# A four-layer fp32 network on one core: layer 3's end with the next batch's scan outputs and the last batch's closing put beside the convolutions

## The chip, the core and the metric

One NeuronCore of one Trainium2 chip runs the whole network in one launch. The metric is the device time of that launch in microseconds. Three runs of the kernel before gave 16581.78, 16579.15 and 16575.54 us (median 16579.15).

## What is computed

The network takes `x` of shape (4, 96, 56, 56) through four layers, each on a normalised input: an attention layer, a layer of selective scans in eight directions, a layer of local top-k similarity with a feed-forward part, and the last one, "layer 3", whose end is changed here. For each of the four batches, layer 3 has four scans `y1..y4` over the image (two along rows, two along columns), each 192 wide per position. Its end, shortened from the reference:

```python
ys = (y1 + y2 + y3 + y4)                      # with Ds added to each
yn = (yn - mu) / jnp.sqrt(var + 1e-05) * ln_g + ln_b      # over the 192
u = jnp.moveaxis(yn, -1, 1) * z               # z: 1x1 projection of the layer's input
t = jax.nn.relu(bn(conv2d(u, c1_w, c1_b), ...))           # 192 -> 384
t = jax.nn.relu(bn(conv2d(t, c2_w, c2_b, groups=2*E, pad=1), ...))   # depthwise 3x3
t = conv2d(t, c3_w, c3_b)                     # 384 -> 96
s = t.mean((2, 3)); s = jax.nn.relu(s @ se1_w.T + se1_b)
s = jax.nn.sigmoid(s @ se2_w.T + se2_b)
return t + t * s[:, :, None, None]            # then added to the network's running x
```

All data are 32-bit floats.

## The kernel before

The four layers run one after the other. `layer3` first calls `into_layer3` (projection and a depthwise convolution) and `cumulative` (the scans, which leave their outputs `ys[0..3]` in DRAM, stored with position as the row and 192 values in a row). Then comes the stage of this document. It works on an image of 56 x 56 = 3136 positions in 7 chunks of 448 (`NCH`, `CH`), each chunk being 4 tiles of 112 positions (`KT`). Batches follow each other strictly, and each has two parts.

`gathered(b)` works with positions on partitions. Per chunk, SP's queue issues six loads for four tiles `y0..y3` (L1495 for the two row scans, L1501, twice each, for the two column scans); VectorE adds the four (L1505) and the constant `dsum` (L1506); `norm_rows` takes statistics (L777, L778), ScalarE a square root (L780), VectorE the reciprocal, the subtraction and multiplication (L784) and the norm's weight and bias (L788, L789). TensorE makes the gate `z` from the layer's input `xn`, which was loaded for the whole image (L1487, L1511); VectorE multiplies (L1512); TensorE transposes (L1516); ScalarE copies the result into `g`, channels on partitions (L1520). The pool of the `y` tiles has 3 buffers of each.

`bottleneck(b)` has NM = 3 tiles `m` of 128 channels. `convolve` runs over these tiles, one ahead: for chunk `c` it issues the depthwise taps of the tile before and the first 1x1 convolution ("fill") of the present tile. Of the nine taps, `on_pe` = 4 are TensorE matmuls with diagonal weights (L417, diagonals made at L403), and the other five are VectorE operations that read the image from SBUF and accumulate in the same PSUM tile (L422). The fill is two matmuls (L1531) and a ScalarE Relu (L1535) into a padded image `xp`; `ended` is a ScalarE Relu from the PSUM tile into `t2` (L1541). After the last tile the third convolution runs (L1557: three matmuls per chunk, L1558), then the mean and the two small matrices with a sigmoid (L1562 to L1572), and the output: VectorE forms `t3 * gate + x` (L1576) with `x` loaded for the whole image before the convolutions (L1524), and GpSimd's queue issues the store (L1577).

What sets the order: inside `in_order` each engine's instructions keep the order of the program text. In the kernel before, this holds for `convolve` only; `gathered` and the end of `bottleneck` are placed by the scheduler. All pools of a batch are opened and closed with it. `convolve` is also used by layers 1 and 3's beginnings, with 4 taps on TensorE there before and after.

Of the kernel before, what the change touches and what calls it, by code (L numbers as in the profile page):

```python
# [17 lines left out]
L = H * W  # L18
# [18 lines left out]
def flat(t):  # L37
    return t.rearrange("p a b -> p (a b)")
# [31 lines left out]
class Net:  # L70
# [319 lines left out]
    def convolve(self, tiles, two, sp, ps):  # L390

        nc = self.nc
        on_pe = 4
        for j in range(len(tiles) + 1):
            now = tiles[j] if j < len(tiles) else None
            old = tiles[j - 1] if j > 0 else None
            if now is not None:
                now["xp"] = two[j % 2]  # L400
                dg = now["dg"] = sp.tile([128, on_pe, 128], F32, name="dg")
                for k in range(on_pe):
                    nc.vector.tensor_scalar(  # L403
                        dg[:, k, :], self.ident, now["weights"][:, k : k + 1], None, ALU.mult
                    )
            for c in range(NCH):
                if old is not None:
                    xp, w = old["xp"], old["weights"]

                    def tap(k):  # L410
                        y = 8 * c + k // 3
                        return xp[:, y : y + 8, k % 3 : k % 3 + W]

                    p = ps.tile([128, 512], F32, name="d")
                    q = p[:, :CH].rearrange("p (h w) -> p h w", w=W)
                    for k in range(on_pe):
                        nc.tensor.matmul(q, old["dg"][:, k, :], tap(k), start=k == 0, stop=k == on_pe - 1)  # L417
                if now is not None:
                    now["fill"](c, now["xp"][:, 1 + 8 * c : 9 + 8 * c, 1 : W + 1])
                if old is not None:  # L420
                    for k in range(on_pe, 9):
                        nc.vector.scalar_tensor_tensor(q, tap(k), w[:, k : k + 1], q, ALU.mult, ALU.add)  # L422
                    old["ended"](c, q)

    def into_scan(self, xin, dram, orders):
# [7 lines left out]
        with ExitStack() as cx:  # L433
# [19 lines left out]
            def tile_of(pr, j):  # L453
# [46 lines left out]
                return dict(weights=cw[:, j, :], fill=fill, ended=ended)  # L500
# [520 lines left out]
    def into_layer3(self, xin, dram):  # L1021
# [4 lines left out]
        with ExitStack() as cx:  # L1026
# [19 lines left out]
            def tile_of(pr, j):  # L1046
# [41 lines left out]
                return dict(weights=cw[:, j, :], fill=fill, ended=ended)  # L1088
# [357 lines left out]
    def layer3(self, xin, xout, dram):  # L1446
# [4 lines left out]
        with ExitStack() as cx:  # L1451
            wp = cx.enter_context(tc.tile_pool(name="ow", bufs=1))
            ga = cx.enter_context(tc.tile_pool(name="og", bufs=1))
            ps = cx.enter_context(tc.tile_pool(name="op", bufs=3, space=PSUM))
            psz = cx.enter_context(tc.tile_pool(name="oz", bufs=1, space=PSUM))
            psd = cx.enter_context(tc.tile_pool(name="od", bufs=3, space=PSUM))
            wz = wp.tile([C, DI], F32, name="wz")
            nc.sync.dma_start(wz, self.d["l3_win"][:, DI : 2 * DI])

            lng, lnb, ds = (self.load_rows(wp, n) for n in ("l3_lnw", "l3_lnb", "l3_d"))  # L1460
            dsum = wp.tile([KT, DI], F32, name="dsum")
# [22 lines left out]
            def gathered(b, g, sp, ss):  # L1484

                xn = sp.tile([C, L], F32, name="xn")
                nc.sync.dma_start(xn, xs[b])  # L1487
                for t0 in range(0, NKT, 4):
                    four = [KT, 4, DI]
                    yk = []  # L1490
                    for k in range(4):
                        y = ss.tile(four, F32, name=f"y{k}")
                        if k < 2:
                            src = ys[k][b, t0 * KT : (t0 + 4) * KT, :].rearrange("(t p) d -> p t d", p=KT)
                            nc.sync.dma_start(y, src)  # L1495
                        else:
                            for r in range(2):
                                src = ys[k][b].rearrange("(w h) d -> w h d", h=H)[
                                    :, 2 * t0 + r : 2 * t0 + r + 7 : 2, :
                                ]  # L1500
                                nc.sync.dma_start(y[r * W : (r + 1) * W], src)  # L1501
                        yk.append(y)
                    acc = yk[0]
                    for k in (1, 2, 3):
                        nc.vector.tensor_tensor(acc, acc, yk[k], ALU.add)  # L1505
                    nc.vector.tensor_tensor(acc, acc, spread(dsum, 4), ALU.add)  # L1506
                    self.norm_rows(acc, lng, lnb, ss)
                    z = psz.tile([KT, 4, 256], F32, name="z")
                    for i in range(4):
                        at = (t0 + i) * KT  # L1510
                        nc.tensor.matmul(z[:, i, :DI], xn[:, at : at + KT], wz, start=True, stop=True)  # L1511
                    nc.vector.tensor_tensor(acc, acc, z[:, :, :DI], ALU.mult)  # L1512
                    for dh in range(2):
                        p = ps.tile([128, 512], F32, name="pn")
                        for i in range(4):
                            nc.tensor.transpose(  # L1516
                                p[:96, i * KT : (i + 1) * KT], acc[:, i, 96 * dh : 96 * dh + 96],
                                self.ident[:KT, :KT],
                            )
                        nc.scalar.copy(g[:, dh, t0 * KT : (t0 + 4) * KT], p[:96, : 4 * KT])  # L1520

            def bottleneck(b, g, sp, s1, ss):
                x = s1.tile([C, L], F32, name="x")
                nc.sync.dma_start(x, xin[b])  # L1524
                t2 = s1.tile([128, NM, L], F32, name="t2")

                def tile_of(m):
                    def fill(c, dst):
                        p = ps.tile([128, 512], F32, name="pn")
                        for dh in range(2):  # L1530
                            nc.tensor.matmul(  # L1531
                                p[:, :CH], c1[:, dh, m * 128 : (m + 1) * 128],
                                g[:, dh, c * CH : (c + 1) * CH], start=dh == 0, stop=dh == 1,
                            )
                        nc.scalar.activation(  # L1535
                            dst, p[:, :CH].rearrange("p (h w) -> p h w", w=W),
                            AF.Relu, bias=s1h[:, m : m + 1], scale=s1c[:, m : m + 1],
                        )

                    def ended(c, p):  # L1540
                        nc.scalar.activation(  # L1541
                            t2[:, m, c * CH : (c + 1) * CH], flat(p),
                            AF.Relu, bias=s2h[:, m : m + 1], scale=s2c[:, m : m + 1],
                        )

                    return dict(weights=c2[:, m, :], fill=fill, ended=ended)

                two = self.padded(s1)
                with in_order(tc):
                    self.convolve([tile_of(m) for m in range(NM)], two, sp, psd)  # L1550
                t3 = s1.tile([C, L], F32, name="t3")
                sums = ss.tile([C, NCH], F32, name="sums")
                for c in range(NCH):
                    cs = slice(c * CH, (c + 1) * CH)
                    p = ps.tile([128, 512], F32, name="pn")
                    for m in range(NM):
                        nc.tensor.matmul(p[:C, :CH], c3[:, m, :], t2[:, m, cs], start=m == 0, stop=m == NM - 1)  # L1557
                    nc.scalar.activation(  # L1558
                        t3[:, cs], p[:C, :CH], AF.Identity, bias=c3b, accum_out=sums[:, c : c + 1]
                    )  # L1560
                mean = ss.tile([C, 1], F32, name="mean")
                nc.vector.tensor_reduce(mean, sums, AX.X, ALU.add)  # L1562
                nc.vector.tensor_scalar(mean, mean, 1.0 / L, None, ALU.mult)
                p = ps.tile([128, 512], F32, name="pn")
                nc.tensor.matmul(p[: DI // 4, 0:1], se1, mean, start=True, stop=True)
                h1 = ss.tile([DI // 4, 1], F32, name="h1")
                nc.scalar.activation(h1, p[: DI // 4, 0:1], AF.Relu, bias=se1b)
                p = ps.tile([128, 512], F32, name="pn")
# [4 lines left out]
                for c in range(NCH):  # L1573
                    cs = slice(c * CH, (c + 1) * CH)
                    o = ss.tile([C, CH], F32, name="o")
                    nc.vector.scalar_tensor_tensor(o, t3[:, cs], gate, x[:, cs], ALU.mult, ALU.add)  # L1576
                    nc.gpsimd.dma_start(xout[b][:, cs], o)  # L1577

            for b in range(B):
                g = ga.tile([96, 2, L], F32, name="g")  # L1580
                with ExitStack() as c2x:
                    sp = c2x.enter_context(tc.tile_pool(name="ob", bufs=1))
                    ss = c2x.enter_context(tc.tile_pool(name="os", bufs=3))
                    gathered(b, g, sp, ss)
                with ExitStack() as c2x:
                    sp = c2x.enter_context(tc.tile_pool(name="tb", bufs=2))
                    s1 = c2x.enter_context(tc.tile_pool(name="t1", bufs=1))
                    ss = c2x.enter_context(tc.tile_pool(name="ts", bufs=3))
                    bottleneck(b, g, sp, s1, ss)
# [141 lines left out]
```

## Time and profile before

| | us |
|---|---|
| median of three runs | 16579.15 |
| the profiled execution | 16544.92 |
| its span | 16543.1 |
| last store of the scans issued | 15721.5 |
| first load of the stage issued (`wz`) | 15722.9 |
| end of the span | 16543.1 |

The stage lasts some 821 us of the span. The page gives busy time over the whole span: TensorE 13366.7 us (81%), VectorE 13918.8 (84%), ScalarE 12240.4 (74%), GpSimd 7665.0 (46%). In the rows, PE is TensorE, DVE VectorE, ACT ScalarE, POOL GpSimd and SP the queue that issues most loads; "PEclk" is the granted clock of TensorE as a share of its full speed. A group row gives the line, engine, operation, tiles written and read, shapes, count, busy time, mean duration of one in ns, and the idle time before it with what ended it. A 32-bit matmul leaves two records in the trace, so "x8" in a row of TensorE is four matmuls.

### The profile page before, as it was taken

How to read it: one execution, taken by the hardware profiler on the slowest of the kernel's cores; microseconds unless marked ns; L12 is line 12 of the kernel's file. 1: busy time of each engine (PE TensorE's matmuls, PEld its weight loads, DVE VectorE, ACT ScalarE, POOL GpSimd, SP SyncE). 2: the span in 40 equal slices, each digit the busy share in tenths (PEclk: the TensorE clock that was granted, in tenths of full speed). 3: DMA queues.
4: the chain of work that ended last, by engine and by line, in shares of the span. 5: the costliest groups of instructions: out<-in, count | busy, mean ns of one | idle time of the engine just before them, and what ended most of it. 6: DMA issues, size and time to landing. Idle time of an engine off the chain costs nothing.

```text
span 16543.1 us, 501276 instructions
## 1 busy us (share of the span) xinstructions
PE 13366.7 (81%) x221976; PEld 8983.6 (54%) x221976; DVE 13918.8 (84%) x15345; ACT 12240.4 (74%) x15452; POOL 7665.0 (46%) x3968
## 2 busy tenths in 40 slices
PE   8999977777777777777776678778888888888866
PEld 4333325666666666666665445446666656666533
DVE  7666549999999999999998777768888888888866
ACT  0465449999999999999996244468888888888822
POOL 0000028888888888888885000023333333333300
PEclk6899889999999999999998588889999999999977
DMA  0000034334444434344445800122212222221122
GB/s 15 1 1 1 16 137 97 91 92 95 105 105 103 103 91 96 92 96 102 103 105 139 194 10 10 43 71 51 50 47 50 50 50 51 51 50 47 43 66 66
DMA packets 821402, 1152.50 MB, mean 70 GB/s; under 512 B 309360, under 2 KB 728720, under 8 KB 807456
## 3 DMA queue, kind: packets, MB, share of 16 engines
q1 hardware_dynamic: 759872, 1055.38, 26.3%
q10 hardware_dynamic: 53984, 45.77, 1.2%
q8 instruction: 1745, 28.59, 0.8%
q0 software_dynamic: 5376, 19.27, 0.4%
q14 instruction: 425, 3.48, 0.1%
HBM read 842.93 MB, written 277.18 MB: 68 GB/s over the span
## 4 chain that ended last, share of the span: by engine, by line
PE 32%; DVE 28%; ACT 19%; issue 15%; DMA 5%; SPq 1%; POOL 1%; DVEq 0%; ACTq 0%; POOLq 0%
DVE q L638 17%; PE q L1357 7%; ACT ht L663 5%; PE s L233 4%; ACT e L626 3%; PE d L417 3%; ACT phi L1305 3%; DVE w L1345 3%; PE z L1297 2%; PE acc L251 2%; PE m L196 2%; ACT w L1313 2%; PE t L561 2%; PE y L675 2%; DVE phi L1366 2%
## 5 line engine op out<-in xcount | busy, mean ns | idle before, releaser
L618 POOL TENSOR_TENSOR q<-du,bm 128x1792 f32<-128x1792 f32 x1344 | 5345.3, 4024 | 3.1 <-DMA bm<-bc 3.1
L638 DVE TENSOR_TENSOR_SCAN q<-e,state,q 128x448 f32<-128x448 f32 x4608 | 4874.1, 1122 | 142.7 <-ACT e L626 140.1
L626 ACT ACTIVATE e<-dl,na 128x448 f32<-128x448 f32 x5376 | 3355.4, 640 | 179.4 <-DVE q L638 123.7
L675 PE MATMUL y<-ht,cd 128*32 128x64 f32 x75264 | 1836.6, 225 | 1480.0 <-ACT ht L663 1479.5
L654 PE MATMUL t<-ident,q 128*128 128x128 f32 x18816 | 2611.9, 292 | 93.9 <-issue 77.8
L1357 PE MATMUL q<-w,m 32*32 32x192 f32 x52224 | 2573.2, 348 | 124.1 <-DVE phi L1366 71.2
L654 PEld LDWEIGHTS t<-ident,q 128*128 128x128 f32 x18816 | 2377.1, 203 | 324.4 <-issue 201.1
L663 ACT COPY ht<-t 128x896 f32<-128x896 f32 x2688 | 2428.3, 903 | 87.1 <-PE t L654 57.1
L675 PEld LDWEIGHTS y<-ht,cd 128*32 128x32 f32 x75264 | 1399.7, 110 | 1958.2 <-ACT ht L663 1942.9
L1357 PEld LDWEIGHTS q<-w,m 32*32 32x32 f32 x52224 | 1873.3, 113 | 737.7 <-issue 184.3
L1366 DVE TENSOR_TENSOR phi<-q,phi 128x768 f32<-128x768 f32 x1632 | 1512.4, 952 | 519.4 <-PE q L1357 491.7
L1378 POOL TENSOR_TENSOR t<-t 128x384 f32<-128x384 f32 x408 | 407.3, 998 | 2974.2 <-DVE t L1377 2974.2
L1297 PE MATMUL z<-ad,sm 32*32 32x256 f32 x39168 | 1277.4, 391 | 396.2 <-ACT phi L1305 382.0
L241 ACT ACTIVATE e<-s 128x896 f32<-128x896 f32 (+1 forms) x1050 | 921.7, 915 | 902.6 <-PE m L196 508.2
L1305 ACT COPY phi<-z 128x1536 f32<-128x1536 f32 x816 | 1164.5, 1427 | 526.5 <-PE z L1297 526.3
L208 DVE TENSOR_REDUCE pm<-m 128x1 f32<-128x448 f32 (+1 forms) x1672 | 982.9, 616 | 667.1 <-PE m L196 599.6
L1345 DVE TENSOR_TENSOR w<-w,misc 128x3072 f32<-128x3072 f32 x408 | 1364.8, 3345 | 82.7 <-PE misc L1329 47.0
L1313 ACT ACTIVATE w<-phi,lntiny,w_k_rmask 128x3072 f32<-128x3072 f32 x408 | 1203.1, 2949 | 2.6
L196 PE MATMUL m<-ka,qa 32*128 32x448 f32 (+1 forms) x3344 | 1169.3, 638 | 7.5 <-DVE pm L208 7.5
L1321 ACT ACTIVATE phi<-phi,w_k_nmask 128x3072 f32<-128x3072 f32 x408 | 1165.5, 2857 | 2.4
L1297 PEld LDWEIGHTS z<-ad,sm 32*32 32x32 f32 x39168 | 708.7, 104 | 659.6 <-ACT phi L1305 463.0
L292 POOL DMA_DIRECT2D x<-xc x28 | 14.5, 517 | 2178.4 <-DVE xc L291 2177.5
(255 smaller groups left out, 18928.9 us busy)
## 6 DMA issues: line engine op xcount, KB each, us to landing
bm<-bc SPq DMA_DIRECT2D x896, 448.0 KB
cm<-cd SPq DMA_DIRECT2D x544, 186.0 KB
l1y<-out SPq DMA_DIRECT2D x672, 96.0 KB
l1y<-out SPq DMA_DIRECT2D x672, 72.0 KB
y<-l1y ACTq DMA_DIRECT2D x224, 168.0 KB
l3y<-y SPq DMA_DIRECT2D x1616, 23.2 KB
w<-l3cr SPq DMA_DIRECT2D x408, 48.0 KB
l3cr<-phi SPq DMA_DIRECT2D x408, 48.0 KB
```

What stands on the lines that cost most here:

```text
L618: nc.gpsimd.tensor_tensor(q, spread(s["du"][:, j, :], ng), s["bm"][g], ALU.mult)
L626: nc.scalar.activation(e[:, :CH], s["dl"][:, j, :], AF.Exp, scale=na[:, s["k"], j, n : n + 1])
L638: nc.vector.tensor_tensor_scan(a, e, a, first, ALU.mult, ALU.add)
L654: nc.tensor.transpose(flat(t)[:, 128 * c : 128 * c + 128], view(q, h * NC2 + c, [[NC, 128]]), self.ident,)
L663: nc.scalar.copy(t, flat(s["t", j, g, h])[:, : NC2 * 128])
L675: nc.tensor.matmul(s["y", j][r : r + 32, c // 4, 64 * half : 64 * half + 64], s["cd"][:, half, g, c, :], s["t", j, g, h][:, 128 * i + 64 * ...
L1297: nc.tensor.matmul(z[32 * b : 32 * b + 32, p, dh].rearrange("p n d -> p (n d)"), s["s"][ps_, dh, b, lo : lo + 32], st["ad"][ps_, dh, 8 * h ...
L1305: nc.scalar.copy(st["phi"][:, :, :, 8 * h : 8 * h + 8, :].rearrange("p a b n d -> p a b (n d)"), z.rearrange("p a b n d -> p a b (n d)"),)
L1313: nc.scalar.activation(w.rearrange("p a n d -> p (a n d)"), st["phi"].rearrange("p a b n d -> p (a b n d)"), AF.Sigmoid, bias=lntiny, scal ...
L1345: nc.vector.tensor_tensor(st["w"], st["w"], ut, ALU.mult)
L1357: nc.tensor.matmul(qp[bs, n, :DI], st["m"][bs, 4 * q + n, :], st["w"][bs, :, 4 * q + n, :], start=True, stop=True,)
L1366: nc.vector.tensor_tensor(ph, view(st[q], 0, [[256, 4], [32, 6], [1, 32]]), ph, ALU.mult)
```

## The change

All of the stage is now one `in_order` region with one set of pools. `gathered(0)` runs alone, as before. Then one call of `convolve` covers the twelve tiles of all four batches (13 rounds of 7 steps), and at each step it calls `before()`, which advances the closing of the batch before, and `beside()`, which advances the shaping of the next batch's scan outputs by one of three parts. The four scans are added by GpSimd. The weight of the norm goes into `wg` and its bias is brought in by one more matmul (`wz` times bias) in the PSUM tile where the transposes land; the transposes are ordinary matmuls with the identity. The subtraction and scaling go to ScalarE. The `y` tiles have 2 buffers, PSUM pools are smaller, and taps on TensorE are 3, 2, 3 for the tiles m = 0, 1, 2 in place of 4. `x` and `xn` are loaded chunk by chunk.

```diff
-    def convolve(self, tiles, two, sp, ps):
+    def convolve(self, tiles, two, sp, ps, before=lambda: None, beside=lambda: None):
...
             for c in range(NCH):
+                before()
                 if old is not None:
-                    xp, w = old["xp"], old["weights"]
+                    xp, w, on_pe = old["xp"], old["weights"], old["on_pe"]
...
                     old["ended"](c, q)
+                beside()
...
-            ps = cx.enter_context(tc.tile_pool(name="op", bufs=3, space=PSUM))
+            ss = cx.enter_context(tc.tile_pool(name="os", bufs=2))
+            ps = cx.enter_context(tc.tile_pool(name="op", bufs=2, space=PSUM))
             psz = cx.enter_context(tc.tile_pool(name="oz", bufs=1, space=PSUM))
-            psd = cx.enter_context(tc.tile_pool(name="od", bufs=3, space=PSUM))
+            pst = cx.enter_context(tc.tile_pool(name="ot", bufs=2, space=PSUM))
+            psd = cx.enter_context(tc.tile_pool(name="od", bufs=2, space=PSUM))
...
+            wg = wp.tile([C, DI], F32, name="wg")
+            nc.vector.tensor_tensor(wg, wz, lng[:C], ALU.mult)
+            nc.vector.tensor_tensor(wz, wz, lnb[:C], ALU.mult)
...
+            def fetch(b, c):
...
+                xn = ss.tile([C, CH], F32, name="xn")
+                nc.sync.dma_start(xn, xs[b][:, c * CH : (c + 1) * CH])
...
+            def added(q):
+                y = q["ys"]
+                nc.gpsimd.tensor_tensor(y[0], y[0], y[1], ALU.add)
+                nc.gpsimd.tensor_tensor(y[2], y[2], y[3], ALU.add)
+                nc.gpsimd.tensor_tensor(y[0], y[0], y[2], ALU.add)
+                nc.gpsimd.tensor_tensor(y[0], y[0], spread(dsum, 4), ALU.add)
+
+            def statistics(q):
...
+                    nc.vector.bn_stats(st[:, i, :], acc[:, i, :])
+                    nc.vector.bn_aggr(mv[:, i, :], st[:, i, :])
...
+                nc.scalar.activation(rs, mv[:, :, 1], AF.Sqrt, bias=self.eps[:KT])
+
+            def normalised(q):
...
+                    nc.tensor.matmul(
+                        z[:, i, :DI], q["xn"][:, i * KT : (i + 1) * KT], wg, start=True, stop=True
+                    )
+                nc.vector.reciprocal(rs, rs)
...
+                nc.vector.scalar_tensor_tensor(nm, mv[:, :, 0], -1.0, rs, ALU.mult, ALU.mult)
+                for i in range(4):
+                    nc.scalar.activation(
+                        acc[:, i, :], acc[:, i, :], AF.Identity,
+                        bias=nm[:, i : i + 1], scale=rs[:, i : i + 1],
+                    )
+
+            def gated(q):
+                acc = q["ys"][0]
+                nc.vector.tensor_tensor(acc, acc, q["z"][:, :, :DI], ALU.mult)
+
+            def turned(q):
...
+                for dh in range(2):
+                    p = pst.tile([128, 512], F32, name="tr")
+                    nc.tensor.matmul(
+                        p[:96, :CH], wz[:, 96 * dh : 96 * dh + 96], q["xn"], start=True, stop=False
+                    )
                     for i in range(4):
...
+                        nc.tensor.matmul(
+                            p[:96, i * KT : (i + 1) * KT], acc[:, i, 96 * dh : 96 * dh + 96],
+                            self.ident[:KT, :KT], start=False, stop=i == 3,
+                        )
+                    nc.scalar.copy(gs[b][:, dh, c * CH : (c + 1) * CH], p[:96, :CH])
+
+            def gathered(b):
+
+                qs = [fetch(b, 0), fetch(b, 1)]
+                added(qs[0])
+                for c in range(NCH + 1):
+                    if c < NCH:
+                        statistics(qs[c])
+                    if c > 0:
+                        turned(qs[c - 1])
+                    yield
+                    if c == NCH:
+                        return
+                    normalised(qs[c])
+                    if c + 1 < NCH:
+                        added(qs[c + 1])
+                    yield
+                    gated(qs[c])
+                    if c + 2 < NCH:
+                        qs.append(fetch(b, c + 2))
+                    yield
...
+                return dict(weights=c2[:, m, :], on_pe=(3, 2, 3)[m], fill=fill, ended=ended)
+
+            def closing(b):
+
                 t3 = s1.tile([C, L], F32, name="t3")
                 sums = ss.tile([C, NCH], F32, name="sums")
+                yield
                 for c in range(NCH):
...
+                        nc.tensor.matmul(
+                            p[:C, :CH], c3[:, m, :], t2[b, m][:, cs], start=m == 0, stop=m == NM - 1
+                        )
                     nc.scalar.activation(
                         t3[:, cs], p[:C, :CH], AF.Identity, bias=c3b, accum_out=sums[:, c : c + 1]
                     )
+                    yield
...
-                    o = ss.tile([C, CH], F32, name="o")
-                    nc.vector.scalar_tensor_tensor(o, t3[:, cs], gate, x[:, cs], ALU.mult, ALU.add)
+                    o = ss.tile([C, CH], F32, name="o", bufs=3)
+                    nc.sync.dma_start(o, xin[b][:, cs])
+                    yield
+                    nc.vector.scalar_tensor_tensor(o, t3[:, cs], gate, o, ALU.mult, ALU.add)
                     nc.gpsimd.dma_start(xout[b][:, cs], o)
...
+                for b in range(B):
+                    coming = closing(b - 1) if b > 0 else iter(())
+                    for _ in range(NM * NCH):
+                        next(coming, None)
+                        yield
+                yield from closing(B - 1)
+
+            ends = ending()
+            outputs = (x for b in range(1, B) for x in gathered(b))
+
+            with in_order(tc):
+                for _ in gathered(0):
+                    pass
+                self.convolve(
+                    [tile_of(b, m) for b in range(B) for m in range(NM)], two, sp, psd,
+                    lambda: next(ends, None), lambda: next(outputs, None),
+                )
+                for _ in ends:
+                    pass
```

## The prediction

> **What bounds the kernel now.** The change lies behind the scans, so I cut the stage first, by the table of windows (per row: length, then busy us and instructions of PE, PEld, DVE, ACT, POOL, then granted clock, DMA share, GB/s).
>
> ```profile
> 15722.00:15807.00 85.00, 29.36 (x111) 25.66 (x112) 65.86 (x161) 9.77 (x23) 0.00 (x0) 0.54 0.57 141
> 15807.00:15924.00 117.00, 113.92 (x301) 56.06 (x299) 73.12 (x114) 38.01 (x61) 0.77 (x8) 0.98 0.05 11
> 16327.00:16410.00 83.00, 29.57 (x114) 25.70 (x115) 66.25 (x152) 10.06 (x22) 2.94 (x12) 0.56 0.58 144
> 16410.00:16524.00 114.00, 112.06 (x297) 54.90 (x295) 72.90 (x111) 36.36 (x58) 0.23 (x3) 0.99 0.04 11
> ```
>
> Shaping (some 84 us a batch) is VectorE's, with TensorE a third busy at half clock; convolving and closing (some 117) is TensorE's. The chain of waits says the same of the second part:
>
> ```profile
> 15879.02 3.01 PE d L417 x8
> 15882.03 1.50 PE pn L1531 x4
> 15883.54 18.04 PE d L417 x48
> 15905.34 15.05 PE pn L1557 x40
> 15935.46 10.02 DMA y<-l3y
> ```
>
> A middle step is 3.01 + 1.50 = 4.51 us of TensorE: 0.75 per tap or per 448-wide matmul. The next batch's first loads start only after the closing, and 10 us of it show. The groups of the stage (the fourth of the whole page) give the prices of what moves:
>
> ```profile
> L1505 DVE TENSOR_TENSOR y<-y,y 112x768 f32<-112x768 f32 x84 | 79.6, 948 | 46.8 <-DMA y<-l3y 46.8
> L784 DVE TENSOR_SCALAR y<-y,mv,rs 112x192 f32<-112x192 f32 x112 | 34.8, 374 | 0.3
> L788 DVE TENSOR_TENSOR y<-y,w_l_lnw 112x768 f32<-112x768 f32 x28 | 26.6, 951 | 0.1
> L1228 POOL TENSOR_TENSOR du<-dl,u 96x752 f32<-96x752 f32 x136 | 244.2, 1796 | 30.2 <-ACT dl L1191 29.8
> ```
>
> Three rows of the timeline (start, length, work, count) give the pace of taps on VectorE, of short matmuls at full clock and of z at half clock:
>
> ```profile
> 15886.65 24.54 DVE L422 SCALAR_TENSOR_TENSOR d<-xp,w_l_c,d 128x448 f32<-128x448 f32 x35 [0.93 <-PE d L417]
> 10002.08 1.20 PE L999 MATMUL misc<-wt,ft 112*96 112x112 f32 x10 [0.52 <-ACT wt L996]
> 15801.55 2.77 PE L1511 MATMUL z<-wz,xn 96*112 96x192 f32 x8
> ```
>
> A tap on VectorE is 24.54 / 35 = 0.70. The stage is 821 us (15722 to 16543); everything else keeps its time.
>
> **Part by part.** *Off VectorE:* per chunk four adds (0.95 each), four L784, L788 and L789: 28 x (3.8 + 1.25 + 1.9) = some 195 us. What stays per chunk: statistics 1.35 (timeline: 0.33 per pair), two tiny operations 0.45, the gate's product 0.95, so 2.75. *On ScalarE:* 112 scalings of 112x192, not shown before; between L780 (112x4, 0.30) and L1193 (96x376, 0.48), I take 0.38: 43 us on an engine that has under 40 of 117 busy; off the path except before the product. *On GpSimd:* 112 adds of 112x768; nearest is L1228, 1.83 after scaling by 768/752, so 7.3 per chunk. *On TensorE:* z at full clock: in the last row above 8 records take 2.4 us at clock 0.54, so 1.3. Turning: two matmuls of 448 (1.5) and sixteen records of L999's very shape, 0.105 warm: 1.7, together 3.2. The other bound is z's 0.16 a record: 4.1, which would add some 0.9 per chunk beside m = 0 and in the chain, 12 x 0.9 = 11 in all; L999 is the nearer shape. At the cold clock I take 0.2 a record and, with the first long matmul done ahead, 4.6 after the product. The two `wg` products (0.36 each by L1462) lie under the first load.
>
> *A step with nothing to wait for.* m = 0 (3 taps on TensorE): per three steps VectorE has 18 x 0.70 + 0.3 + 2.75 = 15.7, TensorE 3 x (2.26 + 1.50) + 1.3 + 3.2 = 15.8: 5.25 a step. m = 1 (2 taps): VectorE 14.7 + 0.3 + 2.75 = 17.7, TensorE 13.5: 5.9. Moving taps to VectorE costs; the shaping under it pays.
>
> *The new chain.* The third convolution of a chunk is issued at the head of the step that follows its last tap tile. Its third matmul waits for that step's `ended`; in TensorE's order the next taps and fill stand behind it. So seven steps of each batch run in series: matmul 0.75, three taps 2.26 + 0.28 to the first VectorE tap, six taps 4.3, `ended` 0.72, handing over 0.15 (my guess; 0 to 0.4 would be 31 x 0.25 = 8 at most) = 8.45. Under it fits the fill, z and the other matmuls (4.3 of 5.2 free); turning overruns by 1.0, twice a batch. Before, these seven convolutions took 15 us a batch, so this is the dear part.
>
> *The loads.* SP now issues seven loads a chunk, the first waiting until the same buffer's earlier chunk is turned; 28 loads of `xn` (before 4) and 28 of `o` (before 4 of `x`) share that queue. From the second batch: 15931.36 to 15942.33 for 1.89 MB, then 1.5 and 1.8 us for the next two 0.344 MB: 2.0 fixed and 0.21 MB/us. So y3 lands 8.6 after release, three adds of GpSimd follow (5.5): 14 us from turned to statistics, on which all of VectorE's taps then wait. Beside m = 0, VectorE reaches them 20 us after the product, which is 17.4 after turning: covered with 3.3 to spare; m = 1, 6.1. Alone, in `gathered(0)`, it is not: turning 4.6, load and adds 14, statistics to product 4.9 = 23.5 per two chunks, against some 17 before. First chunk ready at 15743.5, last turned at 15823.5 (before: 15807); then seven fill steps wait on batch 1's first chunks, and the first tap of VectorE is at about 15850 (before 15823.5).
>
> *Outputs.* `o` is loaded on SP behind such a waiting fetch, twice in batches 1 and 2. It lands some 10 us after turning, VectorE wants it 3 us after: 7 us each, all its taps queued behind; bounds 0 (served at once) and 9. The sigmoid's table (1.28) and `ended` before it hold VectorE 2.3 per batch. At the end each third output waits for a store (2.4, the page's time from issue to landing), then a load: 12.5 from gate to last product, against 7.
>
> *One rule against it:* the Trainium skill, "SBUF — State Buffer", section "Who interferes with whom", says a VectorE instruction with two SBUF inputs and a GpSimd one that reads SBUF exclude each other for a whole instruction. The taps read one image from SBUF and one from PSUM, and layer 1's rows show them with GpSimd copying:
>
> ```profile
> 2292.44 3.59 DVE L422 SCALAR_TENSOR_TENSOR d<-xp,w_l_cw,d 128x448 f32<-128x448 f32 x5 [0.28 <-PE d L417]
> 2294.14 11.46 POOL L494 COPY t<-dup 128x3136 f32<-128x3136 f32 x2
> ```
>
> Five taps take 3.59 there as in the stage without GpSimd. So nothing by the row; by the rule the 28 output products (two SBUF inputs) may each wait up to one add, 1.8; GpSimd is at work two fifths of the time, so an estimate of some 10 us. I take the row and keep 10 for the range.
>
> *The sum,* from 15722: to the first VectorE tap 128; batch 0's 14 steps 7 x 5.25 + 7 x 5.9 + 1.2 of diagonals = 79; batches 1 and 2 each: 5.3, chain 7 x 8.45 + 2 = 61, 6 x 5.25 + 2 = 33.5, 7 x 5.9 + 2.7 = 44 (the additions are output products), diagonals 1.8, loads of `o` 14, sigmoid 2.3 = 162; batch 3, with no shaping left after three steps: 5.3 + 59 + 28 + 38 + 4 = 135; the last tile 4.5 + 6 x 8.45 = 55; to the gate 4.5; outputs 12.5; to the end of the span 10.8 as before. Together 128 + 79 + 324 + 135 + 83 = 749, against 821: 72 us less. The profiled execution would go from 16544.92 to 16473; the median of the runs lies 34 higher, and I carry that over: 16579.15 - 72 = 16507.
>
> **Rivals.** *Better cover* (0.16): `o` is served at once and the sigmoid hides: 28 + 7 less, and fetches 2 us shorter: 3 x 2 less at the start; 113 us gained, 16466. For it: the DMA share is low (0.05) in convolutions. Against: SP's order is fixed.
>
> *Loads eat the gain* (0.16): if turned-to-statistics is longer by x, the stage grows by 3x at the start, 6(x - 3.3) beside m = 0, 7(x - 6.1) beside m = 1 and 4x at `o`. At x = 5 (0.12 MB/us instead of 0.21): 15 + 10 + 20 = 45, so 27 gained, 16552. For it: the 144 GB/s of the shaping windows, though there VectorE set the pace.
>
> *Slower* (0.08): the same loop as the bound, two buffers against three. At x = 8.3, so 22 us from turned to statistics, it costs 105 and the kernel is 0.2% slower; at x = 10, 30 + 40 + 27 + 40 = 137, 65 us slower: 16644. It needs GpSimd's adds at twice L1228's price with loads slowed too. The rows speak against that.
>
> **The numbers.** About 0.2% (33 us) is what can be told from no change. The forecast (33 to 100 us gained) has 0.60, better cover 0.16: faster 0.76; same 0.16; slower 0.08. Low is the better cover, 16466; high is x = 6.5 (19 + 19 + 3 + 26 = 67), 16574, which also holds the 10 of the port.
>
> **What would show it.** Right: seven steps a batch of 8 to 9 us where TensorE's L1557-like matmul waits on ScalarE's `ended`; 5 to 6 us in the others, VectorE above 90% busy there; a start longer by some 25 us; TensorE's clock near full throughout. Wrong: long waits of the statistics for GpSimd beside convolutions, taps above 0.70, adds far from 1.8, waits for `o` other than 4 of about 7.

## The result and the profile after

The changed kernel takes 16519.66 us (median of 7 runs, 16499.88 to 16548.19); the kernel before, measured beside it, 16563.21 (7 runs, 16543.09 to 16581.78). The ratio is 0.9973, with a 95% interval of 0.9962 to 0.9985: some 44 us faster, where 72 were forecast. Part of what brings the median near the forecast 16507 is luck: the kernel before was itself 16 us faster here than in the three runs (16579.15) that the forecast started from. The profiled execution is 16515.64 us long, its span 16513.9.

The layers ahead of the stage are the same program, and their length differs from run to run, so the stage is compared by itself: from SP's issue of the stage's first load to the end of the span. By that cut it is 820 us before (15722.9 to 16543.1) and 785 after (15728.7 to 16513.9): 35 less, where the sum had 72 (749 against 821).

The parts are cut at VectorE's first tap of a tile; the tile in which a batch's third convolutions are spread counts to the batch after it.

| part of the stage, us | forecast | measured |
|---|---|---|
| to VectorE's first tap | 128 | 138 |
| batch 0 | 79 | 79.5 |
| batch 1 | 162 | 168 |
| batch 2 | 162 | 165 |
| batch 3 | 135 | 140 |
| last tile | 55 | 66 |
| gate, outputs, end | 28 | 28 |

Four rows of the table of windows of the changed kernel (length, then busy us and instructions of PE, PEld, DVE, ACT, POOL, then granted clock, DMA share, GB/s): the start, batch 0, six steps in series with shaping, five steps of the last tile.

```profile
15728.50:15866.60 138.10, 76.50 (x287) 51.30 (x288) 38.97 (x127) 33.98 (x74) 72.50 (x48) 0.66 0.53 123
15866.60:15946.10 79.50, 72.66 (x252) 41.34 (x252) 76.06 (x145) 33.01 (x61) 36.19 (x20) 0.96 0.41 94
15954.60:16005.80 51.20, 42.82 (x133) 21.62 (x132) 31.62 (x60) 17.66 (x36) 13.68 (x8) 1.00 0.16 38
16430.40:16481.30 50.90, 32.25 (x61) 13.62 (x60) 20.71 (x31) 7.23 (x15) 0.00 (x0) 0.83 0.00 0
```

Batch 0 is what the change is for: VectorE 76 of 79.5 us busy, GpSimd adding beside it. At the start no engine is busy even 60% of the time. The last two rows are the steps in series. The third row's six steps (one of them with turning) take 8.53 on average, the fourth row's five 10.18, with less work and a clock of 0.83.

The chain of waits in one such step with shaping:

```profile
15958.17 0.70 DVE d L422
...
15958.90 0.73 ACT t L1609
15959.63 0.04 issue
15959.67 0.99 PE pn L1625 x2
15960.66 2.27 PE d L417 x6
...
15963.03 0.70 DVE d L422
```

Last tap, `ended`, the third convolution's last matmul (0.99, shown to its modelled end), three taps, and only then VectorE's first tap: the loop that the prediction wrote down. Groups of the stage:

```profile
L422 DVE SCALAR_TENSOR_TENSOR d<-xp,w_l_c,d 128x448 f32<-128x448 f32 x532 | 365.9, 689 | 137.3 <-PE d L417 121.6
L1544 ACT ACTIVATE y<-y,nm,rs 112x192 f32<-112x192 f32 x112 | 52.0, 536 | 6.0 <-DVE nm L1542 6.0
L1519 POOL TENSOR_TENSOR y<-y,y 112x768 f32<-112x768 f32 x28 | 51.6, 1844 | 2.2
L1527 DVE BATCH_NORM_STATS2 st<-y 112x6 f32<-112x192 f32 x112 | 37.5, 334 | 54.7 <-POOL y L1520 54.7
L1651 DVE SCALAR_TENSOR_TENSOR o<-t,gate,o 96x448 f32<-96x448 f32 x28 | 18.8, 676 | 37.3 <-DMA o<-x 37.2
```

Taps are at 0.69 and an add by GpSimd at 1.84, as forecast. VectorE idles 121.6 us for taps of TensorE, by far its longest wait in the stage, and TensorE's third convolutions idle 65.3 us for `ended`:

```profile
L1625 PE MATMUL pn<-t,w_l_c 128*96 128x448 f32 x168 | 78.4, 580 | 65.3 <-ACT t L1609 65.3
```

The 54.7 us of waiting for GpSimd lie in the start, and 29.2 of the 37.2 for `o` in batches 1 and 2.

### The profile page after: what moved, and what is told of

Same layout as the page of the kernel before. It is cut to its first block, busy times and chain, and to the rows that moved or that the text cites. A ratio compares the mean times of both kernels' runs of the same rounds, so it can differ in the third digit from the quotient of the medians.

```text
span 16513.9 us, 501524 instructions
## 1 busy us (share of the span) xinstructions
PE 13360.2 (81%) x222088; PEld 8967.9 (54%) x222088; DVE 13840.0 (84%) x15191; ACT 12281.5 (74%) x15562; POOL 7866.4 (48%) x4056
## 4 chain that ended last, share of the span: by engine, by line
PE 28%; DVE 26%; issue 21%; ACT 18%; POOL 3%; DMA 3%; SPq 1%; POOLq 0%; DVEq 0%; ACTq 0%
DVE q L639 17%; PE q L1358 5%; ACT ht L664 5%; ACT e L627 4%; PE s L233 4%; PE acc L251 2%; ACT phi L1306 2%; PE m L196 2%; PE z L1298 2%; DVE w L1346 2%; PE y L676 2%; PE d L417 2%; PE t L562 2%; PE t L655 2%; ACT w L1314 1%
```

## Experiments

Theory: the shaping beside the convolutions pays as forecast, but the closing, put at the head of each step, runs it in series, and in the steps where TensorE has least to do, that also lowers its clock. Rivals: the start's two buffers, SP's order of loads, GpSimd's adds, the taps' split. Each run is judged by its ratio to the kernel before (the changed kernel has 0.9973) and by its profiled stage, with the same cut as above (785.2). The stage is that of one profile a run; in the runs that leave them alone, the start (137.4 to 137.9) and batch 0 (79.5 to 79.7) agree within half a microsecond. The intervals of the runs with `o` by ScalarE, idle matmuls, three buffers and four taps overlap the changed kernel's, so for these four the profiled stage carries the comparison.

| run | median us | ratio (95%) | stage us | against 785.2 |
|---|---|---|---|---|
| closing behind the fill | 16443.38 | 0.9928 (0.9914 to 0.9941) | 700.6 | -84.6 |
| `o` by ScalarE | 16503.60 | 0.9958 (0.9945 to 0.9970) | 763.3 | -21.9 |
| idle matmuls | 16512.31 | 0.9966 (0.9953 to 0.9978) | 769.2 | -16.0 |
| three `y` buffers | 16481.27 | 0.9953 (0.9940 to 0.9967) | 747.7 | -37.5 |
| adds on VectorE | 16585.21 | 1.0009 (1.0003 to 1.0016) | 846.5 | +61.3 |
| four taps on TensorE | 16504.65 | 0.9959 (0.9947 to 0.9972) | 762.8 | -22.4 |
| closing in one block | 16471.03 | 0.9939 (0.9927 to 0.9952) | 722.3 | -62.9 |
| combination | 16367.70 | 0.9882 (0.9869 to 0.9896) | 638.8 | -146.4 |
| combination, last batch's taps | 16382.51 | 0.9892 (0.9875 to 0.9908) | 627.5 | -157.7 |

**The closing behind the fill.**

```diff
             for c in range(NCH):
-                before()
                 if old is not None:
...
                 if now is not None:
                     now["fill"](c, now["xp"][:, 1 + 8 * c : 9 + 8 * c, 1 : W + 1])
+                before()
                 if old is not None:
                     for k in range(on_pe, 9):
```

> One move: the third convolution's matmuls are issued behind the step's taps and fill on TensorE, not ahead of them, so that the matmul which waits for `ended` no longer stands in front of the next step's taps. Theory (the serial chain and the clock that it lowers are where 30 of the missing us lie): no step of seven runs in series any more. Chain steps beside shaping go from 8.4 to TensorE's own work, 2.26 + 1.50 + 2.26 + 1.7 = 7.7 (7 each in batches 1 and 2: 10 us), in batch 3 the four steps without shaping from 10.2 to 6.0 (17 us) and three others 0.7 each (2), in the last tile six steps from 10.2 to 4.6 (34 us), with TensorE's clock back at 1.0 there: some 63 us less than the changed kernel, near 16457 us. Rival (the steps are long for another reason, the load on VectorE or ScalarE): the time stays within 10 us of the changed kernel's, and the clock of the last tile at 0.83.

Measured: the stage is 84.6 us shorter, more than the 63 expected; the intervals of the two ratios don't meet. The windows of this kernel, seven steps with shaping, most of batch 3's, and the last tile:

```profile
15944.00:15990.00 46.00, 46.00 (x157) 24.81 (x156) 35.68 (x67) 19.39 (x40) 14.47 (x8) 1.00 0.29 68
16255.00:16299.00 44.00, 44.00 (x130) 21.67 (x129) 31.24 (x50) 18.09 (x35) 0.00 (x0) 1.00 0.00 0
16373.00:16400.00 27.00, 26.15 (x70) 11.87 (x68) 24.79 (x36) 8.11 (x18) 0.00 (x0) 1.00 0.00 1
```

TensorE is busy nearly without a gap and at full clock. Its chain of waits holds, from 15940 to 15990, nothing but TensorE's own work; `ended` is gone from it:

```profile
15959.83 2.26 PE d L416 x6
15962.09 1.51 PE pn L1597 x4
15963.59 2.26 PE pn L1625 x6
15965.85 2.25 PE d L416 x6
15968.11 1.50 PE pn L1597 x4
```

Over the whole stage, the third convolutions wait 1.6 us for `ended`, not 65.3, and VectorE's taps 37.7 us for TensorE's, not 121.6; the difference of 83.9 is nearly all of the gain:

```profile
L1625 PE MATMUL pn<-t,w_l_c 128*96 128x448 f32 x168 | 68.1, 540 | 1.6 <-ACT t L1609 1.6
L422 DVE SCALAR_TENSOR_TENSOR d<-xp,w_l_c,d 128x448 f32<-128x448 f32 x532 | 365.9, 689 | 54.5 <-PE d L416 37.7 <-ACT t L1609 0.9
```

A step without shaping is 2.26 + 1.51 + 2.26 = 6.0, as expected; the steps of the last tile are 4.5. Batch by batch the stage is shorter by some 11 (batch 1), 16, 24 and 34 (last tile). For batch 3 and the last tile 19 and 34 were expected; batches 1 and 2 were taken too low: the eight steps concerned took 55.6 us in batch 1 against 66.5, so 7.0 each where the theory had 7.7, and in batch 2 a first step of 11.3 became one of 5.1. The same move puts ScalarE's copy of each third convolution behind the fill's Relu; what that is worth by itself was not separated. Of all that was tried, the series is the largest loss of the change.

**The closing in one block.**

```diff
-                    for _ in range(NM * NCH):
-                        next(coming, None)
+                    for i in range(NM * NCH):
+                        for _ in range(0 if i < NCH else NCH + 1 if i == NCH else 1):
+                            next(coming, None)
                         yield
+                for _ in range(NCH):
+                    yield
                 yield from closing(B - 1)
```

> One part undone in its order: the seven third convolutions of a batch run in one block, behind the batch's last tap tile, as before the change; the shaping, the gate and the outputs stay beside. Theory (spreading them, one to a step, is what makes the steps run in series): the seven steps take what VectorE or TensorE need, some 5.3 with shaping, 4.3 to 4.5 without, and the block 15.8 us with VectorE idle: batches 1 and 2 some 5 us less each, batch 3 18 less, the last tile (7 x 4.3 + 15.8 = 46 against 66) 20 less, some 48 us less than the changed kernel, near 16472. Rival (spreading is worth its 15 us a batch): 20 us or more longer than the changed kernel.

Measured: the profiled stage is 62.9 shorter where 48 were expected, and the ratios put this run some 56 us ahead of the changed kernel; that the median of 16471.03 met the expected 16472 owes to chance: the kernel before ran 8 us slower beside it. The block in its timeline, 21 matmuls (42 records) at 0.75 each, then the taps that VectorE waits for:

```profile
16006.19 4.70 PE L1625 MATMUL pn<-t,w_l_c 128*96 128x448 f32 x12
16011.14 11.52 PE L1625 MATMUL pn<-t,w_l_c 128*96 128x448 f32 x30 [0.25 <-ACT t L1628]
16022.49 2.42 PE L417 MATMUL d<-xp,dg 128*128 128x448 f32 x6
```

VectorE's taps stop for 15.2 us here (one ends at 16009.7, the next begins at 16024.95; the product and two diagonals fill 3 us of it), and still the stage is shorter than with the convolutions spread over the steps. Spreading them at the step's head costs more than it hides; behind the fill it hides them.

**Keeping TensorE at work.**

```diff
+            def warmed():
+                drawn[0] += 1
+                if next(outputs, done) is not done:
+                    return
+                n = 2 if drawn[0] <= 10 * 7 else 3 if drawn[0] > 12 * 7 else 0
...
+                for _ in range(n):
+                    nc.tensor.matmul(
+                        p[:96, :CH], wz[:, 0:96], gs[B - 1][:, 0, 0:CH], start=True, stop=True
+                    )
```

> Idle matmuls are added where shaping has ended and the closing still runs in series: two of 448 columns at the end of each of the last four chain steps of batch 3, three in each step of the last tile, into a PSUM tile that nobody reads. They are extra work and fill TensorE's idle time. Theory (the steps there are 10.2 and not 8.4 us because TensorE, less busy, is granted a lower clock): clock 0.97 or more in those stretches, waiting matmul and three taps back to 0.99 and 2.42, steps of 8.4 to 8.6, 15 to 18 us less than the changed kernel, near 16503. Rival (the clock follows something else, or the step's length comes from elsewhere): steps stay at 10.2 or grow by the idle matmuls to 11 or more, and the time stays or rises by up to 10 us.

Measured: 16.0 us less in the stage; in the ratio 0.0007, within the intervals. Timeline of TensorE in the last tile, first of the changed kernel:

```profile
16440.29 1.67 PE L1625 MATMUL pn<-t,w_l_c 128*96 128x448 f32 x4
16445.68 1.53 PE L1625 MATMUL pn<-t,w_l_c 128*96 128x448 f32 x2 [3.73 <-ACT t L1609]
16447.00 3.62 PE L417 MATMUL d<-xp,dg 128*128 128x448 f32 x6
```

and then with the idle matmuls (L1679):

```profile
16450.52 2.42 PE L1679 MATMUL tr<-g,wz 96*96 96x448 f32 x6
16452.77 1.67 PE L1625 MATMUL pn<-t,w_l_c 128*96 128x448 f32 x4
16455.92 0.99 PE L1625 MATMUL pn<-t,w_l_c 128*96 128x448 f32 x2 [1.47 <-ACT t L1609]
16456.74 2.42 PE L417 MATMUL d<-xp,dg 128*128 128x448 f32 x6
```

The bracket is the pause: 3.73 us, after which the waiting matmul takes 1.53 and three taps 3.62; with more work and a pause of 1.47 it is 0.99 and 2.42. The window of the same steps has clock 1.00, and they take 8.48 (42.40 / 5) instead of 10.18:

```profile
16442.30:16484.70 42.40, 35.03 (x91) 15.04 (x90) 20.70 (x30) 7.24 (x15) 0.00 (x0) 1.00 0.00 0
```

That the clock costs 1.7 a step here is shown: more work made the step shorter. In batch 3 only the four later steps got idle matmuls, and three of them went from 10.18 to 8.48; its first two, which still have shaping beside them, got none and stayed at 10.1 each.

**Loads of `o` by ScalarE.**

```diff
-                    nc.sync.dma_start(o, xin[b][:, cs])
+                    nc.scalar.dma_start(o, xin[b][:, cs])
```

> The loads of `o` are issued by ScalarE, not by SP. Theory (what VectorE waits for is SP's order: the load stands behind a fetch that waits for its buffer): the five waits of 5 to 7 us in batches 1 and 2, 29 us in all, go to nearly nothing, and the time falls by 25 to 29 us below the changed kernel's, near 16492. Rival (the packets of the fetch themselves are in the way, whichever queue the load is in): waits of 3 us and more stay, and less than 12 us are gained.

Measured: 21.9 less in the stage. The group of output products, here with 11.7 us of waiting against 37.3:

```profile
L1651 DVE SCALAR_TENSOR_TENSOR o<-t,gate,o 96x448 f32<-96x448 f32 x28 | 19.8, 712 | 11.7 <-DMA o<-x 11.5
```

SP's order is the cause, as the theory had it: 25.6 us of waiting are gone, and what stays lies at the end of the kernel, but for one wait of 1.5. The stage gained 4 less than that; 2 of these lie in the end of the kernel, which takes 30.4 us here and 28.3 in the changed kernel. The rest was not followed up.

**Three buffers of `y`.**

```diff
-                    y = ss.tile(four, F32, name=f"y{k}")
+                    y = ss.tile(four, F32, name=f"y{k}", bufs=3)
...
-                qs = [fetch(b, 0), fetch(b, 1)]
+                qs = [fetch(b, 0), fetch(b, 1), fetch(b, 2)]
...
-                    if c + 2 < NCH:
-                        qs.append(fetch(b, c + 2))
+                    if c + 3 < NCH:
+                        qs.append(fetch(b, c + 3))
```

> Three buffers for each of the four `y` and for `xn`, and three chunks fetched ahead, not two. Theory (at the start two buffers tie chunk c + 2 to the turning of chunk c): the cycle of 25.5 us per two chunks becomes some 8 per chunk, the largest of GpSimd's adds 7.3, the loads 7.4 and statistics to product 6.4 + 0.95; chunk 6 is reached some 28 us earlier, and the first tap of VectorE comes 108 to 112 us after the first load, not 138; the convolutions stay as they are, 16490 us. Rival (the loads share the bandwidth and set the cycle, at 0.12 MB per us): 13 us per chunk as now, and no gain beyond 5 us.

Measured: VectorE's first tap comes 107 us after the first load, not 138, and the statistics wait 18.3 us in all, not 54.7. The window of the start and the group:

```profile
15731.79:15838.90 107.11, 67.04 (x287) 47.07 (x288) 43.99 (x128) 34.51 (x74) 77.38 (x51) 0.76 0.76 173
```

```profile
L1527 DVE BATCH_NORM_STATS2 st<-y 112x6 f32<-112x192 f32 x112 | 37.4, 334 | 18.3 <-POOL y L1520 10.1 <-DMA y<-l3y 8.1
```

Of the 37.5 us, 31 lie here. The cycle is 8.6 per chunk (six in 51.6), and 173 GB/s move where 123 did: the loop through two buffers, not the bandwidth, set the start.

**Additions on VectorE.** The four `nc.gpsimd.tensor_tensor` of `added` become `nc.vector.tensor_tensor`.

> One part undone: the four additions of a chunk stand on VectorE again, at the same place of the order. Theory (GpSimd's adds are what pays beside the convolutions): 16 of the 21 chunks of batches 1 to 3 are shaped where VectorE sets the pace; each costs 3.8 us there, 61 together, and the five that fall in steps in series cost 1 to 2 each: 60 to 70 us more than the changed kernel, near 16585, which is no faster than the kernel before. The start stays within 10 us (2.85 instead of 5.5 behind each load, but 3.8 more on VectorE per chunk). Rival (the adds could as well be on VectorE, since the port costs as much as they save): less than 30 us more. The small product for the norm's mean, up to 1.23 us beside GpSimd's adds, should be back at 0.16 if GpSimd is what it waits for.

Measured: 61.3 us more in the stage, as expected, and 0.1% slower than the kernel before (1.0003 to 1.0016): without GpSimd's adds the change as ordered doesn't pay. The run also shows GpSimd's own price. Two groups of small VectorE operations in the changed kernel,

```profile
L1542 DVE SCALAR_TENSOR_TENSOR nm<-mv,rs 112x4 f32<-112x4 f32 x28 | 14.4, 513 | 1.0
L402 DVE TENSOR_SCALAR dg<-ident,w_l_c 128x128 f32<-128x128 f32 x32 | 11.1, 401 | 0.0
```

and with the additions on VectorE:

```profile
L1542 DVE SCALAR_TENSOR_TENSOR nm<-mv,rs 112x4 f32<-112x4 f32 x28 | 4.5, 162 | 1.0
L402 DVE TENSOR_SCALAR dg<-ident,w_l_c 128x128 f32<-128x128 f32 x32 | 7.2, 277 | 0.0
```

All 28 products for the mean take 0.16 here. So some 14 us of VectorE's time (9.9 + 3.9) are waits for GpSimd inside such operations.

**Four taps on TensorE in every tile.** `on_pe=(3, 2, 3)[m]` becomes `on_pe=4`.

> One part undone: four taps on TensorE in every tile of the stage, not 3, 2, 3. Theory: steps with shaping are then TensorE's (3.01 + 1.50 + 1.5 = 6.0) where they are 5.25 and 5.9 now; the steps in series stay at 8.4 (0.75 more on TensorE, 0.70 less on VectorE); in batch 3 without shaping 4.5 against 4.9 and 5.5 gives some 8 us back: 5 to 12 us more than the changed kernel, within 0.1% of it. Rival (a busier TensorE keeps its clock and shortens the steps in series of batch 3 and the last tile): those steps under 9.5 us, and the time 5 to 10 us less than the changed kernel's.

Measured: 22.4 us less, against 5 to 12 more in the theory and 5 to 10 less in the rival: neither had the size. The changed kernel's steps in series of batch 3 (all but the first), then of this run the seven of batch 3, its other fourteen steps, and the last tile:

```profile
16289.70:16347.90 58.20, 47.15 (x117) 21.57 (x116) 26.06 (x39) 13.90 (x26) 0.00 (x0) 0.88 0.00 0
16270.80:16331.50 60.70, 53.08 (x155) 25.74 (x154) 25.96 (x42) 17.68 (x34) 0.00 (x0) 1.00 0.00 0
16331.50:16395.60 64.10, 64.10 (x173) 31.97 (x172) 53.14 (x85) 21.99 (x31) 3.58 (x7) 1.00 0.13 38
16405.80:16456.80 51.00, 35.98 (x71) 15.28 (x70) 17.24 (x25) 7.22 (x15) 0.00 (x0) 0.83 0.00 0
```

The second row keeps clock 1.00 where the changed kernel has 0.88: the rival's mechanism, there but not in the last tile, which stays at 0.83 and 10.2 a step. By parts: batch 0 some 3 longer, batches 1 and 2 together 9 shorter, batch 3 some 16, last tile 1. Of the 16, some 8 are its steps in series and 8 its other steps, as the theory had these; the 9 of batches 1 and 2 are not explained.

**All together.** The first, second and fourth edit, and `on_pe=(3, 2, 2)[m]`.

> The changed kernel with the closing behind the fill, the loads of `o` on ScalarE, three buffers of `y`, and two taps on TensorE, not three, in the tiles of m = 2, where TensorE now sets the pace. By the separate runs: 84 us of the closing's place, 21 to 25 of the loads, 31 to 37 of the buffers in their profiles, and 0.7 for each of 14 steps of batches 1 and 2 by the taps: if they add up, 140 to 150 us less than the changed kernel, near 16375 us. Rival (they cover the same time: the waits for `o` and the steps of the closing hide each other): 100 to 115 us less.

Measured: 16367.70, ratio 0.9882; the stage is 638.8. The three edits had 84.6 + 21.9 + 37.5 = 144 by themselves and the taps some 10 by estimate, so the gains add up but for 8 us and cover different time. Two taps in the tiles of m = 2 help beside shaping (the first such tile takes 41.9 us, against 46.6 with the closing behind the fill alone) and cost in the last tile (34.7, against 32.1).

**And other taps in the last batch.** `on_pe=(3, 2, 2)[m] if b < B - 1 else (4, 4, 3)[m]`.

> The combination before it, with other tap counts for the last batch, which has no shaping beside it: four taps on TensorE for m = 0 and m = 1, three for m = 2. Theory (without shaping a step of n taps costs the larger of 0.75 n + 1.5 on TensorE and 0.70 (9 - n) + 0.7 on VectorE): the seven steps of m = 0 go from 4.8 to 4.5, those of m = 1 from 5.5 to 4.5, those of the last tile from 5.0 to 4.5: some 12 us less than the combination, near 16356 us. Rival (TensorE's and VectorE's handing over costs what the balance gains): within 4 us of it.

Measured: the profiled stage is 11 us shorter (627.5), but only 7.5 of them lie in the last batch and its last tile: the tile of m = 1 is 5.7 shorter, the last tile 3.8, and that of m = 0 is 1.7 longer. The other 4 lie in the start and in batch 1, which this edit leaves alone. So about two thirds of the 12 are shown; the whole is 16382.51, with an interval (0.9875 to 0.9908) that overlaps the combination's. In its profile the unchanged layers ahead took 31 us longer (15756.1 against 15725.2), so which of the two is faster stays open. Either is some 135 to 150 us ahead of the changed kernel by the ratios.

## Why the prediction was right in sign and too large

**Right.** The closing runs in series, as forecast: seven steps a batch, 8.41 without turning against 8.45. Batch 0 79.5 against 79, an add 1.84 against 1.83, waits for `o` 29.2 in all against 28, though they are five of 5 to 7 (three in batch 1, two in batch 2) and not four of 7, the end as summed. From product to the next statistics at the start 18.8 against 18.6. Beside the convolutions no statistics waited for GpSimd, so "loads eat the gain" and its slower extreme are out; "better cover" is out as well, since the `o` loads did wait behind SP's fetch, which the run with ScalarE's loads shows by removing it. The row of z shows 2.77 us for its eight records, where the sum read 2.4; in the changed kernel the eight take 1.46 at full clock, and the next matmul starts after 1.30, as summed. The terms of batch 3 add up to 134, not 135; nothing hangs on it.

**The step that failed: "TensorE's clock near full throughout", and with it the term "6 x 8.45" of the last tile and the "59" of batch 3's series.** I took the price of a step from one at full clock and carried it to all. In the last tile TensorE pauses 3.73 us in each step, the granted clock is 0.83, and the step is 10.18; in batch 3 five of the seven steps take 10.1 to 10.2, at a clock of 0.88, with pauses of 2.2 in most. The last tile came out 11 longer (66 for 55), batch 3's seven steps 9 longer (68.4 for 59.2; the rest of batch 3 came out 4 shorter). Eleven slow steps at 1.7 are 19 us; the idle matmuls reach nine of them and give 16 back. The clock was not near full in batches 1 and 2 either: the first step in series of batch 2 is 11.3, as TensorE pauses 7.82 us before its matmul and three taps then take 4.52.

The Trainium skill, "TensorE: Matmul & The Clock Gate", section "Part 1: The HAM clock gate", has TensorE fall to half clock after an idle window of about 3.4 us; by that page a pause of 8.45 - 2.26 - 2.26 = 3.9 in the last tile could have been read from my own sum. The trace agrees with it for 3.73 against 1.47, but shorter pauses also go with a lower clock. The first row is the run with four taps, last tile (pause 3.00); the other two are the changed kernel, batch 3 (pause 2.23, three taps at 3.95), while in batch 1 a pause of 2.22 (before the matmul at 15959.67 in the chain above) goes with 0.99 and, in the timeline, three taps at 2.42:

```profile
16410.22 1.25 PE L1625 MATMUL pn<-t,w_l_c 128*96 128x448 f32 x2 [3.00 <-ACT t L1609]
16332.71 1.20 PE L1625 MATMUL pn<-t,w_l_c 128*96 128x448 f32 x2 [2.23 <-ACT t L1609]
16333.71 3.95 PE L417 MATMUL d<-xp,dg 128*128 128x448 f32 x6
```

So the length of a pause alone does not tell the clock here. What else decides stays open.

**A term too small: the start,** 10 us. A cycle of two chunks is 25.5, not 23.5: statistics take 1.95, not 1.35 (here each second operation waits for the first), the four scalings 1.86, not 1.5, and the small product for the norm's mean 0.91, not 0.16, beside GpSimd's adds; so statistics to product is 6.4, not 4.9. Three cycles make 6 us of it, the first and the last chunk the rest. The buffers, which the prediction named as the loop, decide it: a third one gives 31 us back.

**A term set to zero: the port.** I took the taps' row, and the taps indeed stay at 0.69, but the section cited in the prediction (the Trainium skill, "SBUF — State Buffer", "Who interferes with whom") holds here for operations that it names: those with two SBUF inputs, and `tensor_scalar`, which makes the diagonals. The product for the norm's mean (two small SBUF inputs) goes from 0.16 to as much as 1.23, a diagonal from 0.28 to as much as 1.91. The output products, for which I had weighed it, stay at 0.67 to 0.68; where one meets an add, it is GpSimd's add that takes 2.2 to 2.3 instead of 1.8 (in the run with ScalarE's loads one product, at 16214.51, was the one to wait: 1.76). So some 14 us of VectorE. Of these, 0.75 in each cycle of the start lies on the path; how much does in batches 1 to 3 was not separated. Batches 1 and 2 were 6 and 3 us longer than summed, of which the step of 11.3 explains 3; the rest is not taken apart.

**A choice that the sum did not question.** "So this is the dear part" was right, but I priced the series only against itself. In one block the same convolutions cost 63 less, behind the fill 85 less. And "moving taps to VectorE costs; the shaping under it pays": undone, the kernel is 22 us faster, so on the whole it didn't pay here: it gained 3 us in batch 0, where there is shaping in every step and no closing, and lost 16 in batch 3, where nearly all steps have no shaping left. Of the change's parts the adds on GpSimd are worth 61 us. The norm's weights in the gate were not tried by themselves.

## What to carry to other kernels

Where each engine keeps the order of the text, put work that waits for another engine's result behind, not ahead of, what that other engine needs next: one call moved within the step was worth 84.6 us of the stage, more than the 35 of the whole change. Before trusting a step's price, ask whether TensorE will have the granted clock there that it had where the price was taken: the same step cost 8.48 at full clock and 10.18 at 0.83. And a prefetch depth is counted in stages of the loop: two buffers made one cycle out of load, addition, normalising and turning.

## What was not expected of the hardware

Adding idle matmuls made a step shorter: 10.18 to 8.48 with six records more, as the granted clock went from 0.83 to 1.00. A VectorE operation on four elements per partition takes up to 1.23 us beside GpSimd's additions and 0.16 in the run without them, while a tap of 448 with an operand in PSUM is untouched at 0.69.
